# Block 0 of a retention and feed-forward kernel: constants on another queue, rounding units and weight additions in other places, two tiles centred on VectorE

## The chip, the core and the metric

The kernel runs on one core of one Trainium2 chip. A core has TensorE (PE, matmuls, with a sequencer row PEld for weight loads), VectorE (DVE), ScalarE (ACT), GpSimd (POOL) and SyncE (SP), each with its own in-order instruction stream, and 16 DMA engines that serve queues written by SP and ACT. The metric is the device time of one launch in microseconds: the median of several runs. Lower is better.

## The reference

The input is x, 4 sequences of 1024 tokens with 512 features, so 4096 tokens, all float32. Two sandwiched sublayers follow, each wrapped in layer norms without gain:

```python
x = x + LN(attn(LN(x)))
x = x + LN(ffn(LN(x)))

# attn: 16 heads of 32, lam per head
q, v, g = x @ Wq.T, x @ Wv.T, silu(x @ Wg.T)
ret[t]  = lam * ret[t-1] + v[t]              # a scan along the sequence
out     = (LN(q * ret) * gamma + beta) * g
return out @ Wo.T

# ffn: 512 -> 1536 -> 512, weights rounded to float8_e4m3
h = silu((x @ f8(gate_w)) * gate_scale) * ((x @ f8(up_w)) * up_scale)
return (h @ f8(down_w)) * down_scale
```

## The kernel before, in words

**Blocks.** The 4096 tokens are worked through in eight blocks of 512 (t = 0 to 7), each of four tiles of 128 tokens (s = 0 to 3). `Retention` is the attention part of a block, `Ffn` its feed-forward part. The feed-forward loop runs 12 steps (i = 0 to 11) per block: `gate(i)` and `up(i)` are eight matmuls each (`pfg`, `pfu`), `fuse` and `rest` split the product into two parts, `down` adds it into four sums (`pd`). Woven into the steps of block t is the attention part of block t+1 (`b` in the code) and the input of block t+2 (`n`). Every instruction is written in a fixed order per engine and kept in it: the helper `InOrder` records all of them, so the profile gives one line, L74, to all; they are told apart by the names of tiles.

**The first 90 us** are block 0's attention part (`a`), which has no feed-forward work to hide behind. SP and ACT load x in halves, ACT then loads beta and the other constants (`load_const`), SP loads Wv, Wq (`load_square`), four pieces of feed-forward weights, Wg, block 1's x and Wo. On ACT the activation table is loaded behind these issues, and `keep_x` copies the transposed tiles `ptx` to `xnT`, from which the v products (`pv`) start. A DMA takes one of eight semaphores in turn and waits for the DMA eight before it.

**Rounding.** The feed-forward weights are rounded to float8 on the chip, in 18 pieces, from the start until step 7 of block 0. For each piece VectorE takes the exponent bits (`unit`, 128x1024), ScalarE turns them into a rounding constant with two activations (`units()`, a pair), and VectorE adds and subtracts it (`finish`). `rounds(n)` takes n of these VectorE steps; `now=False` leaves the pair of activations to the next call of `units()`. A pair that stands early in ScalarE's order waits for its unit and holds up what is behind it; one that stands late holds up the addition.

**Block 1's statistics.** In step 3 of block 0, `halves()` splits the sum over features (ScalarE the upper half, VectorE the rest), `mean()` multiplies it by ones (`mu`), `center_y()` subtracts and squares, POOL adds the squares (`sqsum`). In step 4 `halves()` and `var()` do the same for the variance (`var`), ScalarE takes the root (`rstd`, with a table load before it), and VectorE the reciprocal. `g_of(c)` is a gate product `pg` with silu.

**x1.** For each tile s, in steps 7 to 11: `o(s)` is the output product (`po`); `o_moments` takes mean and variance (VectorE) and the root (POOL); `x1_of` centres and scales `po` into `x1n`, POOL adds x, SP stores the sum (`kept`); `x1_moments` and `x1n_of` norm it again. Centring goes through `self.center`: `shift_scale` is three ScalarE instructions, `center_scale` is one VectorE instruction. Tiles 0 to 2 of block 1 are then transposed by VectorE blockwise (`xs`), stored by SP in four parts (`mxs`) and fetched back (`x1n<-mxs`); tile 3 is transposed by TensorE (`pt`). `upper_of` (ScalarE) and `rest_of` (VectorE) split the transposed tile into the two parts of `x1nT` that the next block's `pfg` and `pfu` read.

**Weight sums.** From block 2 on, the products with Wv, Wq, Wg go by seven half-size products instead of eight, which need sums of quarters of the weights. `weight_sums(k)` makes them in place with four VectorE additions, `keep_sums(k)` stores the four results to DRAM with four DMAs (`dsum_v`, `dsum_q`, `dsum_g`). Before, this goes in steps 8, 9, 10 for v, q, g: additions ahead of the step's `gate`, stores at its end. When the weights are stored, their places are taken by other tiles: `w_ring` (four slots, filled by `fetch_weights`) lies where `wv_sb` was, `t_sums` (POOL's sums of inputs) where `wq_sb` was, `mids` (intermediate results) where `wg_sb` was. The first product of block 2 is made in step 11 (`product`), the second and third at its end; the first one's result is copied by ScalarE into `mids`, and the third adds into the same bank of results.

The orders that matter for the change, from the end of step 11 in ScalarE's stream: the upper part of tile 2, the cast of `fuse_11`, the copy to `mids`, the upper part of tile 3.

Of the kernel before, what the change touches and what calls it, by code (L numbers as in the profile page):

```python
# [15 lines left out]
ALU = mybir.AluOpType  # L16

P = 128
# [5 lines left out]
def retention_ffn_sandwich(  # L24
# [20 lines left out]
    NT, D = x.shape  # L45
    I = gate_w.shape[1]
    NC = D // P
    NI = I // P
    TB = 512
    NS = TB // P  # L50
# [15 lines left out]
    class InOrder:  # L66


        def __init__(self, engine):
            self.engine = engine  # L70
# [5 lines left out]
    pe, dve, act, pool, sp = (  # L76
        InOrder(e) for e in (nc.tensor, nc.vector, nc.scalar, nc.gpsimd, nc.sync)
    )


    def load_x(t, s, queues):
        xt = xpool.tile([P, D], F32, tag="x", name=f"x_{t}_{s}")
        w = D // len(queues)
        for h, queue in enumerate(queues):
            queue.dma_start(xt[:, ts(h, w)], x[ds(t * TB + s * P, P), ts(h, w)])
        return xt

    x_first = [load_x(0, s, [sp, act]) for s in range(NS)]

    def load_const(src, cols, name):  # L90
        t = const.tile([P, cols], F32, tag=name, name=name)
        act.dma_start(t, src)
        return t

    def load_square(src, name):
        w = wpool.tile([P, NC, D], F32, tag=name, name=name)
        v = src.rearrange("(c p) f -> p c f", p=P)
        for h in range(2):
            sp.dma_start(w[:, 2 * h : 2 * h + 2, :], v[:, 2 * h : 2 * h + 2, :])
        return w  # L100

    beta_sb = load_const(beta, NC, "beta_sb")
    wv_sb = load_square(wvT, "wv_sb")
    wq_sb = load_square(wqT, "wq_sb")
    gamma_sb = load_const(gamma, NC, "gamma_sb")
    lnb_sb = load_const(lnb, NC, "lnb_sb")
    gs_sb = load_const(gate_s, NI, "gs_sb")
    us_sb = load_const(up_s, NI, "us_sb")
    ds_sb = load_const(down_s.to_broadcast([P, D]), D, "ds_sb")


    gate_sb = wpool.tile([P, NC, I], F32R, tag="gate_sb", name="gate_sb")
# [102 lines left out]
    def units():  # L215

        while open_units:
            _, c = open_units.pop(0)
            act.activation(c, c, AF.Relu, bias=neg_low)
            act.activation(c, c, AF.Identity, scale=1.5 * 2.0**20, bias=low_unit)  # L220

    def rounds(n, now=True):
        for _ in range(n):
            next(rounding, None)
            if now:
                units()
# [110 lines left out]
    H = TB // 2  # L337
# [4 lines left out]
    squares = {"v": (wvT, wv_sb), "q": (wqT, wq_sb)}  # L342
    operands = {}

    def weight_sums(k):

        src, w = squares[k]
        v = src.rearrange("(c p) f -> p c f", p=P)
        a11, a12, a21, a22 = (w[:, i : i + 2, o : o + H] for o in (0, H) for i in (0, 2))
        operands[k] = {1: v[:, 0:2, 0:H], 2: v[:, 2:4, 0:H], 4: v[:, 2:4, H:D]}  # L350
        dve.tensor_tensor(a22, a21, a22, ALU.add)
        dve.tensor_tensor(a21, a11, a21, ALU.subtract)
        dve.tensor_tensor(a11, a22, a11, ALU.subtract)
        dve.tensor_tensor(a12, a12, a11, ALU.subtract)
        return {5: a22, 7: a21, 6: a11, 3: a12}

    def keep_sums(k, done):
        for j, t in done.items():
            operands[k][j] = dram.tile([P, 2, H], F32, tag=f"sum_{k}{j}", name=f"dsum_{k}{j}", bufs=1)
            sp.dma_start(operands[k][j], t)  # L360

    RING = 4
# [3 lines left out]
    def fetch_weights():  # L366
        n = fetched[0]
        if n < total_products:
            k, j = order[n % len(order)]
            sp.dma_start(w_ring[:, n % RING], operands[k][j])  # L370
            fetched[0] += 1

    class Retention:


        def __init__(self, t, xt=None):
            self.t = t
            self.xt = xt or [load_x(t, s, [sp]) for s in range(NS)]
            self.mv = small.tile([P, NS, 2], F32, tag="mv4", name=f"mv4_{t}", bufs=2)
            self.pv, self.pq, self.pg, self.ret, self.g = {}, {}, {}, {}, {}  # L380
            self.po, self.mvo, self.x1n, self.ptx, self.kept = {}, {}, {}, {}, {}
            self.center = shift_scale if t < 2 else center_scale
            self.fast = t >= FAST
            self.made = 0

# [278 lines left out]

        def x1_of(self, s):
            self.x1n[s] = work.tile([P, D], F32, tag="tok", name=f"x1n_{self.t}_{s}", bufs=4)
            self.center(self.x1n[s], self.po.pop(s), self.mvo[s])
            pool.tensor_tensor(self.xt[s], self.xt[s], self.x1n[s], ALU.add)
            self.kept[s] = dram.tile([P, D], F32, tag="kept", name=f"kept_{self.t}_{s}")
            sp.dma_start(self.kept[s], self.xt[s])  # L670
# [2 lines left out]
            self.mvo[s] = moments(self.xt[s])  # L673

        def x1n_of(self, s):
            self.center(self.x1n[s], self.xt[s], self.mvo.pop(s))

        def new_x1nT(self):

# [162 lines left out]
        load_piece(n)  # L842
    wg_sb = load_square(wgT, "wg_sb")
    squares["g"] = wgT, wg_sb
    a = Retention(0, x_first)
    a.new_xnT()
    warm(14)
# [113 lines left out]
    a.rest_of(1)  # L961
    b.y_of(0)
    a.rest_of(2)
    rounds(3, now=False)
    a.turn_x1n(3)
    a.upper_of(3)
    b.q(2, "pd0", early)
    units()
    a.rest_of(3)
    b.y_of(1)  # L970


# [3 lines left out]
    for t in range(NB):  # L976
        f, n = Ffn(a), None
        fast = b is not None and b.fast
        for i in range(NI):
# [28 lines left out]
                n.shift()  # L1008
            if b and not fast and i == 5:
                b.z(0)  # L1010
            if b and i >= 8:
                b.x1_moments(i - 8)
            if t == 0 and 8 <= i < 11:
                done = weight_sums("vqg"[i - 8])
            f.gate(i)
            if t == 0 and i in (5, 6):
                n.norm_x(2 * i - 10, True)
# [19 lines left out]
            if b and not fast and i == 3:  # L1037
                b.halves()
                units()
                rounds(3, now=False)  # L1040
                b.g_of(0)
                b.mean()
                b.center_y()
                n.stats(3)
                n.rstd()
                n.shift()
            if b and not fast and i == 4:
                b.halves()
                rounds(3, now=False)
                b.g_of(1)  # L1050
                b.var()
            if b and not fast and i == 5:
# [78 lines left out]
                n.fetch_x()  # L1131
            if b and n and i == 11:
                b.rest_of(3)
            if t == 0 and 8 <= i < 11:
                keep_sums("vqg"[i - 8], done)

            if i == f.lag:
                f.sums()
# [25 lines left out]
                n.stats(1)  # L1164
            if t == 0 and i == 9:
                w_ring = wpool.tile([P, RING, 2, H], F32, tag="wv_sb", name="w_ring")
                for _ in range(RING):
                    fetch_weights()
            if t == 0 and i == 10:
                t_sums = wpool.tile([P, 4, 2, H], F32, tag="wq_sb", name="t_sums")  # L1170
# [76 lines left out]
```

## Time and profile before

| what | value |
|---|---|
| median of 6 runs | 985.28 us (984.5 to 987.72) |
| the profiled execution, its own time | 985.25 us |
| its span (first to last instruction) | 983.4 us |
| TensorE busy | 98% |
| VectorE, ScalarE, POOL busy | 68%, 38%, 27% |
| TensorE busy, 0 to 25 us | 23.28 of 25 |
| VectorE busy, 25 to 75 us | 47.36 of 50 |
| DMA moved | 110.07 MB, 112 GB/s |
| granted TensorE clock, mean | 0.995 |

The profile is one execution. A line of the timeline reads: start in us, duration in us, engine, operation, output and input tiles, shape, count, and in brackets the idle time of the engine before it and what ended it. An SPq line is a DMA issue: its duration is that of the issue, not of the transfer. A line of waits reads: who waited, for whom, total us, times, longest. TensorE's work is counted in pairs of records for float32 matmuls, and ends of matmuls are modelled.

### The profile page before, as it was taken

To read this page: it belongs to the slowest core of one execution; us is meant where nothing else is said; L and a number is where in the kernel's file an instruction comes from. 1 tells how busy PE (TensorE), PEld (TensorE's weight loads), DVE (VectorE), ACT (ScalarE), POOL (GpSimd) and SP (SyncE) were. 2 spreads that over 40 slices of the span, in tenths; PEclk is the share of its full clock that TensorE was granted. 3 is DMA by queue.
4 is the path that set the end of the run, shared out by engine and by line. 5 is a ranking of instruction groups with operands and counts; after the bars stand their busy time and mean duration, and the time that the engine had idled before them with its cause. 6 is when DMAs were issued, how large, how long until landed. Compare 5 with 4: busy or idle time off the path is not lost.

```text
span 983.4 us, 11259 instructions
## 1 busy us (share of the span) xinstructions
PE 964.8 (98%) x3950; PEld 735.6 (75%) x3950; DVE 664.5 (68%) x1019; ACT 369.7 (38%) x556; POOL 265.2 (27%) x346
## 2 busy tenths in 40 slices
PE   9999999999999999999999999999999999999996
PEld 7455766678776888678876788768887788867885
DVE  5996979655666667665686666766667765656535
ACT  3556565466645125221432215321152211522323
POOL 1405121412324033240513305133142312322020
PEclk9999999999999999999999999999999999999998
DMA  9312323752416426263232623245241542213021
GB/s 305 112 65 72 121 65 93 212 177 75 150 53 153 128 81 229 78 142 123 86 129 91 177 76 117 87 132 151 82 150 59 134 139 79 72 43 107 1 86 43
DMA packets 90936, 110.07 MB, mean 112 GB/s; under 512 B 8064, under 2 KB 55424, under 8 KB 90880
## 3 DMA queue, kind: packets, MB, share of 16 engines
q1 hardware_dynamic: 89296, 108.43, 36.2%
q10 hardware_dynamic: 1584, 0.94, 0.3%
q8 instruction: 31, 0.51, 0.2%
q14 instruction: 25, 0.20, 0.1%
HBM read 76.56 MB, written 32.77 MB: 111 GB/s over the span
## 4 chain that ended last, share of the span: by engine, by line
PE 82%; DVE 8%; ACT 4%; POOL 2%; DMA 2%; issue 1%; SPq 1%; ACTq 0%; DVEq 0%; POOLq 0%
PE pfu L74 15%; PE pfg L74 15%; PE pd L74 15%; PE pv L74 10%; PE pq L74 9%; PE pg L74 9%; PE po L74 8%; DVE scr L74 1%; DVE st L74 1%; POOL x L74 1%; POOL mv L74 1%; ACT x1n L74 1%; DVE gate L74 1%; DMA xnT<-mx 1%; DVE xs L74 1%
## 5 line engine op out<-in xcount | busy, mean ns | idle before, releaser
L74 PE MATMUL pfu<-x1nT,up_sb 128*128 128x512 f32 x768 | 212.5, 419 | 0.0
L74 PE MATMUL pfg<-x1nT,gate_sb 128*128 128x512 f32 x768 | 195.2, 396 | 0.4 <-DVE x1nT L74 0.4
L74 PE MATMUL pd<-down_sb,fuse 128*128 128x512 f32 x720 | 186.9, 401 | 0.0
L74 PEld LDWEIGHTS pfu<-x1nT,up_sb 128*128 128x128 f32 x768 | 145.2, 189 | 42.5 <-issue 12.9
L74 PEld LDWEIGHTS pfg<-x1nT,gate_sb 128*128 128x128 f32 x768 | 144.2, 188 | 30.4 <-DVE x1nT L74 0.8
L74 PEld LDWEIGHTS pd<-down_sb,fuse 128*128 128x128 f32 x720 | 135.3, 189 | 27.6
L74 ACT CAST fuse<-gate 128x512 fp32r<-128x512 f32 x90 | 55.7, 619 | 235.0 <-DVE gate L74 235.0
L74 ACT ACTIVATE gate<-pfg,gs_sb 128x512 f32<-128x512 f32 x96 | 65.7, 684 | 195.0 <-PE pfg L74 194.9
L74 DVE SCALAR_TENSOR_TENSOR gate<-pfu,us_sb,gate 128x512 f32<-128x512 f32 x96 | 71.8, 748 | 73.7 <-PE pfu L74 71.2
L74 PE MATMUL po<-wo_sb,y 128*128 128x512 f32 x256 | 114.5, 592 | 0.0
L74 POOL TENSOR_SCALAR mv<-mv 128x1 f32<-128x1 f32 (+1 forms) x82 | 19.4, 237 | 300.6 <-DVE mv L74 299.6
L74 PEld LDWEIGHTS po<-wo_sb,y 128*128 128x128 f32 x256 | 48.2, 189 | 50.3 <-issue 46.6
L74 DVE TENSOR_TENSOR fuse<-gate,fuse 128x512 fp32r<-128x512 f32 x90 | 75.2, 835 | 12.4 <-ACT fuse L74 12.4
L74 POOL TENSOR_TENSOR ysum<-y 128x256 f32<-128x256 f32 (+1 forms) x14 | 14.0, 998 | 190.0 <-DVE y L74 190.0
L74 POOL TENSOR_TENSOR x<-x,x1n 128x512 f32<-128x512 f32 x32 | 46.8, 1461 | 45.7 <-DVE x1n L74 36.8
L74 DVE BATCH_NORM_STATS2 st<-x 128x6 f32<-128x512 f32 x64 | 43.6, 682 | 14.0 <-POOL x L74 11.2
L74 POOL TENSOR_TENSOR mv<-mv,nhalf 128x1 f32<-128x1 f32 (+1 forms) x75 | 46.1, 615 | 6.2
L74 PE MATMUL pg<-t_sums,w_ring 128*128 128x256 f32 x192 | 45.7, 381 | 0.6 <-ACT mids L74 0.6
L74 PE MATMUL pv<-t_sums,w_ring 128*128 128x256 f32 x192 | 45.3, 379 | 0.0
L74 PE MATMUL pq<-t_sums,w_ring 128*128 128x256 f32 x192 | 45.3, 379 | 0.0
L74 PEld LDWEIGHTS pg<-t_sums,w_ring 128*128 128x128 f32 x192 | 35.9, 189 | 7.4 <-ACT mids L74 2.2
L74 PEld LDWEIGHTS pv<-t_sums,w_ring 128*128 128x128 f32 x192 | 36.3, 189 | 5.7
(150 smaller groups left out, 1336.9 us busy)
## 6 DMA issues: line engine op xcount, KB each, us to landing
kept<-x SPq DMA_DIRECT2D x32, 256.0 KB, 2.1
x<-kept SPq DMA_DIRECT2D x32, 256.0 KB, 3.9
x<-in_x SPq DMA_DIRECT2D x28, 256.0 KB, 4.3
out<-d SPq DMA_DIRECT2D x27, 256.0 KB, 2.1
xnT<-mx SPq DMA_DIRECT2D x24, 256.0 KB, 4.7
w_ring<-dsum_v SPq DMA_DIRECT2D x24, 256.0 KB, 2.6
w_ring<-dsum_q SPq DMA_DIRECT2D x24, 256.0 KB, 2.6
w_ring<-dsum_g SPq DMA_DIRECT2D x24, 256.0 KB, 2.6
```

The source lines that it names most:

```text
L74: return lambda *args, **kwargs: tc.keep_in_program_order(op(*args, **kwargs))
```

## The change

Four things are moved, all in block 0's time; the number of matmuls and of additions is the same.

1. The loads of gamma, the norm's beta, the two scales and the down scale (`gamma_sb`, `lnb_sb`, `gs_sb`, `us_sb`, `ds_sb`) go from ACT's queue, where they stood before ACT's first work, to SP's queue, behind Wg and before block 1's x. The retention's beta stays on ACT.
2. Of the three rounding steps before the transpose of tile 3 of block 0, the last (a subtraction) goes behind `a.rest_of(3)`. In steps 3 and 4 of block 0 one more `units()` stands behind `rounds(3)`: the pair of the unit just taken is written before `g_of(0)`, mean and centring in step 3, and before `g_of(1)` and `var` in step 4, where it stood behind them.
3. The 12 additions for weight sums are drawn from one generator: 4 in step 8, 6 in step 9, 2 in step 10, there before `x1_moments(2)`. The g sums are stored at once in step 10 and no longer at its end, so the four DMAs stand before the stores of tile 2's blocks on SP. The ring's first four loads are issued two in step 9 and two in step 10.
4. In block 1, tiles 2 and 3 are centred by `center_scale` on VectorE, both in `x1_of` and in `x1n_of`; tiles 0 and 1 stay on ScalarE.

```diff
-    def load_const(src, cols, name):
+    def load_const(src, cols, name, queue=None):
         t = const.tile([P, cols], F32, tag=name, name=name)
-        act.dma_start(t, src)
+        (queue or sp).dma_start(t, src)
         return t
...
-    beta_sb = load_const(beta, NC, "beta_sb")
+    beta_sb = load_const(beta, NC, "beta_sb", act)
     wv_sb = load_square(wvT, "wv_sb")
     wq_sb = load_square(wqT, "wq_sb")
-    gamma_sb = load_const(gamma, NC, "gamma_sb")
-    lnb_sb = load_const(lnb, NC, "lnb_sb")
-    gs_sb = load_const(gate_s, NI, "gs_sb")
-    us_sb = load_const(up_s, NI, "us_sb")
-    ds_sb = load_const(down_s.to_broadcast([P, D]), D, "ds_sb")
...
-    def weight_sums(k):
-        src, w = squares[k]
...
-        dve.tensor_tensor(a22, a21, a22, ALU.add)
-        dve.tensor_tensor(a21, a11, a21, ALU.subtract)
-        dve.tensor_tensor(a11, a22, a11, ALU.subtract)
-        dve.tensor_tensor(a12, a12, a11, ALU.subtract)
-        return {5: a22, 7: a21, 6: a11, 3: a12}
+    def weight_sums():
+        for k, (src, w) in squares.items():
...
+            made[k] = {5: a22, 7: a21, 6: a11, 3: a12}
+            dve.tensor_tensor(a22, a21, a22, ALU.add)
+            yield
+            dve.tensor_tensor(a21, a11, a21, ALU.subtract)
+            yield
+            dve.tensor_tensor(a11, a22, a11, ALU.subtract)
+            yield
+            dve.tensor_tensor(a12, a12, a11, ALU.subtract)
+            yield
+
+    made = {}
+    adding = weight_sums()
...
-            self.center = shift_scale if t < 2 else center_scale
+            self.center = [shift_scale if t < 1 or t < 2 and s < 2 else center_scale for s in range(NS)]
...
     wg_sb = load_square(wgT, "wg_sb")
     squares["g"] = wgT, wg_sb
+    gamma_sb = load_const(gamma, NC, "gamma_sb")
+    lnb_sb = load_const(lnb, NC, "lnb_sb")
+    gs_sb = load_const(gate_s, NI, "gs_sb")
+    us_sb = load_const(up_s, NI, "us_sb")
+    ds_sb = load_const(down_s.to_broadcast([P, D]), D, "ds_sb")
...
-    rounds(3, now=False)
+    rounds(2, now=False)
     a.turn_x1n(3)
     a.upper_of(3)
     b.q(2, "pd0", early)
     units()
     a.rest_of(3)
+    rounds(1, now=False)
     b.y_of(1)
...
+            if t == 0 and i == 10:
+                for _ in range(2):
+                    next(adding)
+                keep_sums("g")
             if b and i >= 8:
                 b.x1_moments(i - 8)
-            if t == 0 and 8 <= i < 11:
-                done = weight_sums("vqg"[i - 8])
+            if t == 0 and i in (8, 9):
+                for _ in range(4 if i == 8 else 6):
+                    next(adding)
             f.gate(i)
...
             if b and not fast and i == 3:
                 b.halves()
                 units()
                 rounds(3, now=False)
+                units()
                 b.g_of(0)
...
             if b and not fast and i == 4:
                 b.halves()
                 rounds(3, now=False)
+                units()
                 b.g_of(1)
                 b.var()
...
-            if t == 0 and 8 <= i < 11:
-                keep_sums("vqg"[i - 8], done)
+            if t == 0 and i in (8, 9):
+                keep_sums("vq"[i - 8])
...
             if t == 0 and i == 9:
                 w_ring = wpool.tile([P, RING, 2, H], F32, tag="wv_sb", name="w_ring")
-                for _ in range(RING):
+            if t == 0 and i in (9, 10):
+                for _ in range(RING // 2):
                     fetch_weights()
```

More of the change, by code (lines that the diff above doesn't have):

```diff
@@ L343, in retention_ffn_sandwich, with keep_sums @@
     operands = {}
-    def weight_sums(k):
-        src, w = squares[k]
-        v = src.rearrange("(c p) f -> p c f", p=P)
-        a11, a12, a21, a22 = (w[:, i : i + 2, o : o + H] for o in (0, H) for i in (0, 2))
-        operands[k] = {1: v[:, 0:2, 0:H], 2: v[:, 2:4, 0:H], 4: v[:, 2:4, H:D]}
-        dve.tensor_tensor(a22, a21, a22, ALU.add)
-        dve.tensor_tensor(a21, a11, a21, ALU.subtract)
-        dve.tensor_tensor(a11, a22, a11, ALU.subtract)
-        dve.tensor_tensor(a12, a12, a11, ALU.subtract)
-        return {5: a22, 7: a21, 6: a11, 3: a12}
-    def keep_sums(k, done):
-        for j, t in done.items():
+    def weight_sums():
+        for k, (src, w) in squares.items():
+            v = src.rearrange("(c p) f -> p c f", p=P)
+            a11, a12, a21, a22 = (w[:, i : i + 2, o : o + H] for o in (0, H) for i in (0, 2))
+            operands[k] = {1: v[:, 0:2, 0:H], 2: v[:, 2:4, 0:H], 4: v[:, 2:4, H:D]}
+            made[k] = {5: a22, 7: a21, 6: a11, 3: a12}
[9 more added lines that the diff above has]
+    adding = weight_sums()
+    def keep_sums(k):
+        for j, t in made[k].items():
             operands[k][j] = dram.tile([P, 2, H], F32, tag=f"sum_{k}{j}", name=f"dsum_{k}{j}", bufs=1)
@@ L666, in x1_of @@
             self.x1n[s] = work.tile([P, D], F32, tag="tok", name=f"x1n_{self.t}_{s}", bufs=4)
-            self.center(self.x1n[s], self.po.pop(s), self.mvo[s])
+            self.center[s](self.x1n[s], self.po.pop(s), self.mvo[s])
             pool.tensor_tensor(self.xt[s], self.xt[s], self.x1n[s], ALU.add)
@@ L675, in x1n_of @@
         def x1n_of(self, s):
-            self.center(self.x1n[s], self.xt[s], self.mvo.pop(s))
+            self.center[s](self.x1n[s], self.xt[s], self.mvo.pop(s))
         def new_x1nT(self):
```

## The prediction

> **What bounds the kernel now.** I read the page first, then the list of what TensorE waited for, then all engines in order of time from 120 to 205 us, then the same places of a later block, which already runs part of what the change does.
>
> From the page, the busy times:
>
> ```profile
> PE 964.8 (98%) x3950; PEld 735.6 (75%) x3950; DVE 664.5 (68%) x1019; ACT 369.7 (38%) x556; POOL 265.2 (27%) x346
> ```
>
> TensorE is the bound nearly everywhere. An edit in block 0 can only win idle time of TensorE there; the work behind it moves as one. TensorE's waits from 0 to 205 us (total, times, longest):
>
> ```profile
> PE pt L74 <- ACT x1n L74: 2.4, 2, 2.1
> PE pv L74 <- ACT xnT L74: 1.8, 2, 1.2
> PE var L74 <- ACT half L74: 1.4, 1, 1.4
> PE pv L74 <- ACT mids L74: 1.1, 1, 1.1
> ...
> PE pfg L74 <- DVE x1nT L74: 0.4, 1, 0.4
> PE var L74 <- DVE half L74: 0.2, 1, 0.2
> ```
>
> That is some 7 us, of which the change touches 5.8 (0.68, 0.37, 1.60, 2.08, 1.09). The places in order of time, from the timelines of TensorE, ScalarE, SyncE and TensorE again (start, duration, work, idle before and its releaser):
>
> ```profile
> 9.39 1.99 PE L74 MATMUL pv<-xnT,wv_sb 128*128 128x256 f32 x8 [0.68 <-ACT xnT L74]
> ...
> 95.63 1.88 PE L74 MATMUL pfg<-x1nT,gate_sb 128*128 128x512 f32 x7 [0.37 <-DVE x1nT L74]
> ...
> 129.88 0.50 PE L74 MATMUL var<-half,mean_r 128*128 128x512 f32 x1 [1.38 <-ACT half L74]
> ...
> 134.91 3.34 DVE L74 RECIPROCAL rstd<-rstd 128x512 f32<-128x512 f32 x1
> ...
> 190.72 1.91 SPq L74 DMA_DIRECT2D mxs<-xs  x4
> 195.05 0.34 SPq L74 DMA_DIRECT2D x1n<-mxs  x1
> ...
> 195.91 3.05 SPq L74 DMA_DIRECT2D dsum_g<-wg_sb  x4
> ...
> 197.13 0.66 PE L74 MATMUL pt<-ident,x1n 128*128 128x128 f32 x4 [2.08 <-ACT x1n L74]
> ...
> 201.84 0.58 ACT L74 COPY mids<-pv 128x512 f32<-128x512 f32 x1 [2.87 <-DMA w_ring<-in_wvT]
> ```
>
> Between 90 and 165 us VectorE is nearly full (9.83 of 10 us in 150 to 160), so a gain of TensorE there lives on only if VectorE's chain comes earlier too. The last line names a load, but `mids` lies where `wg_sb` was: the copy waits for the four stores of the g sums to land (last issue about 197.9, 3.6 us to landing). After 202.5 us TensorE's small waits (0.64 at 253, 0.28 at 315) follow from its own results, so what is won or lost by 202.5 us is won or lost for the whole.
>
> **The change, part by part.** Times are those of the profiled execution: span 983.4, own time 985.25, 0.03 under the median 985.28, so differences carry over as they are.
>
> *Constants' loads.* Five issues leave ScalarE's queue, where they run from 4.51 to 6.85 and hold up the table load (6.88, 1.28 us) and with it the first two copies (1.05 us from 8.29). Now the table load follows beta at about 4.2, the second copy starts at the end of its transpose (7.66+0.60=8.26) and takes 0.53, and `pv` starts at 8.85 for 9.39: 0.54 us won. On SP the five (0.33 to 0.44 each, 2.0 in sum) stand ahead of block 1's x, first read at 37.1 and loaded by then with 10 us to spare (issued by 18.6, at most 9.6 to landing); the constants are read from 58 us on. SP also loses a wait of 2.8 us for beta, which held Wq back to 8.27. TensorE has no gap from there to 50, so the 0.54 stays.
>
> *`rest_of(3)` before the last subtraction.* It now starts when its upper half is copied (93.93) instead of 94.89. The eight `pfg` matmuls take 94.87 to 97.51, 2.64 us, against 1.81 undisturbed: 0.85 won. Behind it `y_of(1)` ends 0.26 later (96.35), which nobody awaits: `gate_0` waited 0.31 for TensorE. TensorE is then 1.39 early, and VectorE, which waited 0.99 and 0.31 for it, follows by 107 us.
>
> *Rounding pairs in block 1's steps 3 and 4.* A pair is 1.13+1.15 us on ScalarE. In step 3 it fills a hole (ScalarE idle 3.23 before the squares): the unit is out at 118.25, the pair ends at 120.55, silu at 121.1, the first square starts at 121.29 as y allows. The cast that waited behind the old pair goes ahead, the upper half of the sum is made at 126.65, bound by POOL's three additions (128.04 less 1.39), and `var` starts at 127.3 for 129.88: TensorE is 2.6 early. It also ran at half clock just behind that gap (0.50 in 132 to 134), some 1.3 us. [...] In step 4 the new pair stands *ahead* of silu, table load and root: unit 128.55, pair to 130.9, silu 131.4, table 132.7, root 133.4. The reciprocal, which nothing else would hold after `gate_4` (131.6), starts at 133.4 for 134.91. VectorE's chain keeps only 1.5, and the half clock falls inside what VectorE makes TensorE wait anyway: `gate_5`'s silu (142.35 for 143.85) releases `pfg_6`.
>
> *Additions 4, 6, 2 for 4, 4, 4.* Four take 2.84, so 0.71 each. With 1.5 won the moments of x1 tile 1 end at 174.8, six additions at 179.05, and the transpose of tile 1 goes at 179.05 for 179.29: 1.25 of the 1.5 is spent.
>
> *Centring tiles 2 and 3 on VectorE.* ScalarE's three steps (0.20+0.29+0.78) and its waits go; VectorE gets two of 0.80 and two of 0.55, counting from a later block:
>
> ```profile
> 428.52 0.80 DVE L74 TENSOR_SCALAR x1n<-po,mv 128x512 f32<-128x512 f32 x1
> ...
> 429.84 1.78 DVE L74 TENSOR_TENSOR fuse<-gate,fuse 128x512 fp32r<-128x512 f32 x1
> ...
> 433.39 1.47 DVE L74 TENSOR_SCALAR x1n<-x,mv 128x512 f32<-128x512 f32 x1 [0.95 <-POOL mv L74]
> ```
>
> The second and third show the price: beside POOL's x addition (429.40 to 431.07) a 0.69 us operation takes 1.78, and beside POOL's `t_sums` the 0.55 centring takes 1.47. Working on: po_2's moments 179.7, gate 181.2, cast 181.9, `rest_9` 182.5, centring 183.3, POOL's x 185.0; the two g additions are caught behind it, to 186.3 (uncaught 185.2). Then moments of tile 2 at 186.3 (were 184.77), centring to 188.7, transpose, po_3 at 189.4, `rest_10` 191.65, centring 193.0, POOL to 194.7, moments, centring 196.55 to 198.0 beside `t_sums`. So `pt` goes at 198.05, not 197.13, and the second product behind it, 4.1 us of TensorE later, at 202.1. [...]
>
> *The g sums' stores ahead of tile 2's blocks.* The wait of 1.09 us goes: the stores are issued by 192.9 and land by 196.5. But SP is a queue: stored x1 of tile 2 (185.0), four q stores (2.90), two ring loads (1.49), four g stores (3.05), so tile 2's block stores go at 192.9 for 190.72. From there to the fetch took 3.94 and 4.33 in this stage and 6.39 in a later block; at 4.33, the row with the same stores before it, the fetch is issued at 197.2 and lands 2.8 later, 200.0 (was 197.83). On ScalarE the upper half of tile 2 waits for it, and behind that stand `fuse_11` (0.53), the `mids` copy (0.58) and tile 3: 0.6+0.53+0.58 puts `pv` at 201.75 for 202.48. The third and fourth ring loads, issued behind the fetch at 198, land by 201.8 and are just in time.
>
> **Sum.** Two chains meet at 202: `pt` and its followers 202.1, `mids` 201.8. The later sets it: 202.1 less 202.48, -0.4 us, 984.9. [...] Bounds: with the catching at nothing (1.1 at the additions, 0.9 at the last centring) `pt` goes at 196.05, and at 3.94 to the fetch the second chain gives 201.35: -1.1. With 6.39 it is 203.9, +1.4. If the first 0.54 fails because Wv's second half (up to 10.1) holds `pv`, add 0.5.
>
> **The rivals.** *Faster: both chains carry the 1.5 to the end.* It needs the additions and centrings free beside POOL, and SP through early: tile 2's x stored at 183.3, blocks at 191.2, fetch 195.1 landing 197.9, `mids` 199.65, and `pt` at 195.6 with its product at 199.7: -2.8, 982.5. For it: ScalarE's six small steps and their waits on POOL are gone, and in 166.97 to 169.8 the additions ran at 0.71 beside POOL's small operations. Against it: the rows of 1.78 and 1.47. If TensorE kept all it won by 142 us (2.75) and lost both waits (2.08, 1.09) too, 5.9 would be won, 979.4; VectorE's chain forbids that.
>
> *Slower: SP's queue.* Its place is the g stores ahead of tile 2's blocks. At the slowest single issue (1.10, four are 4.4 for 3.05) and 6.39 to the fetch, the second chain comes 3.4 later, at 205.2: +2.7, 988.0. It decides once tile 2 lands after 202.7, 4.9 later than before. For it: these stores and loads put 2.5 MB into the queue within 7.5 us, 333 GB/s, and the transfers there already move some 340. Against: the stores before tile 1's blocks left 3.94.
>
> *No effect:* the edits act, but waits they leave stand in the same place; that is the forecast's neighbourhood.
>
> **How the numbers follow.** 0.2% is 1.97 us, about what a measurement of this kernel tells from no change. Forecast within it 0.44 (983.3 to 987.2; its own range 983.9 to 986.7), faster 0.36, slower 0.20. The faster share is large because each estimate leans on contention rows that need not recur at the same overlap; the slower share is the queue and a half clock (1.3 us) behind TensorE's gap before 202, now some 2 us. Range 981.8 to 987.6: it cuts about 0.1 off each side.
>
> **What would show it.** Right: the table load near 4.2 and `pv` near 8.85; no gap before `pfg` at 95; `var` near 127.3 and the reciprocal near 133.4; transpose of tile 1 near 179; block stores of tile 2 near 193; `mids` waiting behind tile 2's upper half, not behind the g stores; `pv`'s wait gone to that or to `pt`. Wrong: tile 2 landing by 198, or `pt` before 196 (then faster); `mids` after 204 (slower); a TensorE gap after 205 that was not there.

## The result, and the profile after

The changed kernel took 987.63 us (median of 18 runs, 986.47 to 988.92) where the kernel before took 985.21 (36 runs, 984.35 to 987.72): ratio 1.0023, 95% interval 1.0017 to 1.003. It is slower by 2.4 us between the medians. The forecast was 984.9 with a range to 987.6, so the time lies just outside it and on the wrong side. The profiled execution of the changed kernel took 986.88, span 984.9. It is 0.75 under its kernel's median, so its trace shows 1.6 of the 2.4 us.

TensorE's busy time is what it was, as the page's first part says:

```profile
PE 964.5 (98%) x3950; PEld 735.1 (75%) x3950; DVE 668.7 (68%) x1023; ACT 365.0 (37%) x544; POOL 266.7 (27%) x346
```

ScalarE lost 4.7 us of work and VectorE gained 4.2. So the loss is idle time of TensorE, or matmuls at a lower clock. TensorE's waits from 0 to 205 us in the changed kernel (total, times, longest):

```profile
PE pt L74 <- DVE x1n L74: 3.4, 1, 3.4
PE pfu L74 <- DVE gate L74: 1.7, 1, 1.7
PE pfg L74 <- ACT gate L74: 1.4, 1, 1.4
PE pv L74 <- ACT xnT L74: 1.4, 2, 1.2
...
PE var L74 <- ACT half L74: 0.6, 1, 0.6
```

Four of the waits aimed at are shorter or gone (`var` 0.6 for 1.4, `pv` 1.4 for 1.8, `pfg` behind the rest of tile 3, `mids`), and three long ones have come in their place. All three wait for VectorE or ScalarE in the stretch from 142 to 200 us. The last of them, in the timeline of TensorE:

```profile
192.11 2.12 PE L74 MATMUL pfu<-x1nT,up_sb 128*128 128x512 f32 x8 [1.73 <-DVE gate L74]
...
199.38 1.09 PE L74 MATMUL pt<-ident,x1n 128*128 128x128 f32 x4 [3.43 <-DVE x1n L74]
200.12 3.05 PE L74 MATMUL pd<-down_sb,fuse 128*128 128x512 f32 x8
203.01 1.89 PE L74 MATMUL pv<-t_sums,w_ring 128*128 128x256 f32 x8
204.74 1.89 PE L74 MATMUL pv<-xnT,w_ring 128*128 128x256 f32 x8
```

`pt` starts 2.25 us later than before, and the four transposes take 1.09 for 0.66, the eight `pd` 3.05 for some 2.1. The windows say why (columns: window, length, TensorE busy, granted clock, DMA share, GB/s):

```profile
196.00:198.00 2.00, 0.00 (x0) 1.00 0.31 81
198.00:200.00 2.00, 0.61 (x3) 0.69 0.82 262
200.00:202.00 2.00, 2.00 (x8) 0.50 0.73 212
202.00:204.00 2.00, 2.00 (x10) 0.95 0.52 186
```

The clock was halved behind the gap. Before, all four windows stand at 1.00. So the last product of block 0 (the third, `pv` from `xnT`, which waited for `mids` before) starts at 204.74 for 202.48, 2.26 later. A wait of 0.28 at 315 us is gone afterwards, which leaves 1.85, and 1.5 in the span.

**Where the early gains went.** TensorE is 0.85 early at `pfu_1`, the up product of step 1 (104.89 for 105.74), and 1.14 early from 154 to 188. Up to 0.44 of either is no gain of the change: x landed that much earlier in this execution (VectorE's first work on it starts at 3.37 for 3.81). VectorE is not early. Its reciprocal:

```profile
132.25 0.75 DVE L74 SCALAR_TENSOR_TENSOR gate<-pfu,us_sb,gate 128x512 f32<-128x512 f32 x1
134.83 3.35 DVE L74 RECIPROCAL rstd<-rstd 128x512 f32<-128x512 f32 x1 [1.83 <-ACT rstd L74]
```

It starts 0.08 earlier than before, although the product in front of it is 2.0 earlier: it now waits 1.83 for the root. ScalarE's stream at that place shows what the root stands behind:

```profile
129.97 1.15 ACT L74 ACTIVATE scr<-scr,neg_low 128x1024 f32<-128x1024 f32 x1 [1.36 <-DVE scr L74]
131.16 1.16 ACT L74 ACTIVATE scr<-scr,low_unit 128x1024 f32<-128x1024 f32 x1
132.22 0.58 ACT L74 ACTIVATE g<-pg 128x512 f32<-128x512 f32 x1
132.81 1.28 ACT L74 ACT_TABLE_LOAD   x1
134.11 0.69 ACT L74 ACTIVATE rstd<-var,eps_sb 128x512 f32<-128x512 f32 x1
```

The first two lines are the pair that step 4 now writes ahead. From there VectorE is where it was before (147.92 for 147.99 at the next addition), with two more additions to make ahead of tile 1's transpose and four more centrings ahead of `pt`.

The theory to be tested (A in the expectations) had three parts: the pair of step 4 spends what was won early; additions and centring then push `pt` back on VectorE; and TensorE, which had stayed early, makes a gap of it that lowers its clock. The main rival was the one of the forecast, SP's queue.

### The profile page after: what moved, and what is told of

It reads as the page before. It is cut to its first block, busy times and chain, and to the rows that moved or that the text cites. A ratio compares the mean times of both kernels' runs of the same rounds, so it can differ in the third digit from the quotient of the medians.

```text
span 984.9 us, 11255 instructions
## 1 busy us (share of the span) xinstructions
PE 964.5 (98%) x3950; PEld 735.1 (75%) x3950; DVE 668.7 (68%) x1023; ACT 365.0 (37%) x544; POOL 266.7 (27%) x346
## 4 chain that ended last, share of the span: by engine, by line
PE 87%; DVE 7%; ACT 2%; POOL 1%; DMA 1%; issue 1%; SPq 0%; ACTq 0%; DVEq 0%; POOLq 0%
PE pfu L74 16%; PE pfg L74 16%; PE pd L74 16%; PE pq L74 10%; PE pv L74 10%; PE po L74 10%; PE pg L74 9%; DVE scr L74 1%; DVE st L74 1%; PE pt L74 1%; DVE fuse L74 1%; DMA wv_sb<-in_wvT 1%; POOL sqsum L74 1%; DVE y L74 1%; DVE d L74 1%
```

## The experiments

All times are medians beside runs of the kernel before on the same chip (985.4 to 985.7 in the three sets); the ratios are to those, with 95% intervals. The start of the kernel shifts by up to a microsecond between profiled executions: x lands at 3.37 to 3.81, and the wait for Wv differs. So the reciprocal of the changed kernel's own stream lies between 134.83 and 135.80 in the variants that leave the first 150 us alone. Places are therefore compared by the distance between two instructions of one execution.

**Undoing the centring.**

```diff
-self.center = [shift_scale if t < 1 or t < 2 and s < 2 else center_scale for s in range(NS)]
+self.center = [shift_scale if t < 2 else center_scale] * NS
```

> The changed kernel with tiles 2 and 3 centred on ScalarE again; the rest of the change stays. Theory A (the loss is made by VectorE's chain in steps 9 to 11, half of it by the centring, and is doubled by a half clock behind a TensorE gap of 3.43 us): the transpose pt goes at 198.4 for 199.38, so 986.6 if the half clock stays (0.50 behind the gap) and 985.2 if the shorter gap (2.4 us) leaves the clock full. Theory B (SP's queue, with the g stores ahead of tile 2's blocks, holds the end): the third product does not move, 987.6.

Measured: 986.15, ratio 1.0004 (0.9996 to 1.0013). `pt` at 198.34 behind a gap of 2.32, clock 1.00 there, so most of the loss is gone. But the third product came at 203.55, behind a new wait of 0.97. The fetch of tile 2 was issued only at 198.32 (197.26 in the changed kernel) and landed by 201.4. The profile puts the wait down to ScalarE's upper part of tile 3, done at 203.51, right behind the `mids` copy (203.02); the ring load issued behind the fetch landed at 203.41. All three stand behind that fetch, so SP's queue does then become the bound, one step after VectorE's.

**Undoing the moved additions and stores.**

```diff
-            if t == 0 and i == 10:
-                for _ in range(2):
-                    next(adding)
-                keep_sums("g")
...
-            if t == 0 and i in (8, 9):
-                for _ in range(4 if i == 8 else 6):
+            if t == 0 and 8 <= i < 11:
+                for _ in range(4):
```

(The stores go back to the ends of the steps, the four ring loads to step 9.)

> The changed kernel with additions, g stores and ring loads where they stood before (four additions in each of steps 8, 9, 10, stores at the steps' ends); centring of tiles 2 and 3 stays on VectorE. Theory A (centring on VectorE beside POOL costs most): x1 moments of tile 2 go at 185.2, pt at 199.0, the wait for mids comes back behind it, 987.0. Theory B (the two extra additions and SP's queue are the loss): 985.3, pt at 198 or before.

Measured: 988.17, ratio 1.0018 (1.001 to 1.0027): nothing is won. `pt` stands 64.05 behind the reciprocal, 0.50 less than in the changed kernel, but behind a gap of the same length (3.42), and the half clock lasted 6.8 us in this profile. The wait for `mids` that theory A expected did not come.

**Leaving out the pair of step 4.**

```diff
                 b.halves()
                 rounds(3, now=False)
-                units()
                 b.g_of(1)
                 b.var()
```

> The changed kernel without the extra pair of step 4, so root and table load no longer stand behind it on ScalarE. Theory A (the early gains of 1.1 us are lost at the reciprocal, which starts at 134.83 for 134.91 since the root waits for that pair): the reciprocal goes at 132.9, gate_5's silu 1.9 earlier, TensorE's wait of 1.40 before pfg_6 goes, VectorE's chain and pt come 1.9 earlier, 985.7. Theory B (VectorE is full from 150 to 170 or waits for POOL and DMA there, so nothing early arrives): pt stays at 199.4, 987.6.

Measured: 985.16, ratio 0.9995 (0.9986 to 1.0004), 2.5 us under the changed kernel. The reciprocal starts at once behind its product, and the wait of 1.4 for `gate_5` is gone. By its start (133.86) it is 0.97 earlier, which looks like half of what I expected, but this execution was 0.95 later already at `pfu_1` and at `var` (129.61 for 128.66), ahead of the edit. From `var` to the reciprocal it takes 4.25 where the changed kernel takes 6.17: the pair costs 1.92, as expected, and `pt` keeps it (92.61 behind `pfu_1` for 94.49). That is most of the 2.5 between the medians. `pt` waited 3.42 in this profile too, but the clock behind it was 1.00.

**Filling the gap.** Small matmuls of constants, into the bank that `pt` overwrites; the first variant did it in six blocks, the second in block 0 only:

```diff
                 n.product()
-                b.turn_x1n(3, "pf")
+                if t == 0:
+                    pt = ps_tile("pt1_fill", "pf")
+                    for _ in range(14):
+                        pe.matmul(pt[:, :P], mean_w, mean_w, start=True, stop=True)
...
```

> The changed kernel with 14 small matmuls of constants (128x128) in TensorE's gap before pt, written to the bank that pt then overwrites; they do not touch any result. Theory A (the clock falls to 0.50 at 198.6 because of the gap and stretches the transposes, pd and pv): pt stays at 199.4, the clock behind it is 1.00, pd takes 2.1 for 3.05, 986.3. Theory B (pd is stretched by something else, such as late weights): the clock and pd stay as they are, 987.6 or more.

Measured: 1000.63, ratio 1.015 (1.0135 to 1.0165). The edit was wrong: 14 matmuls take 3.29 us, and five later blocks have no gap to put them in. In block 0 itself the run did what theory A said (third product at 203.76, clock 1.00).

> The changed kernel with the 14 small matmuls of constants before pt in block 0's step 11 only (the run with them in six blocks paid some 3.3 us for each of the later five). Theory A (behind the gap of 3.43 us the clock falls to 0.50 in most executions, and costs 1.0): third product at 203.8 for 204.74, 986.6, clock 0.998, and executions that lie closer together. Theory B (the clock is an accident of one execution): 987.5, spread as it was (986.5 to 988.9).

Measured: 986.29, ratio 1.0007 (0.9999 to 1.0016), 11 runs from 986.04 to 987.43, mean clock 0.997 or 0.998 in each. TensorE in this run:

```profile
196.41 3.29 PE L74 MATMUL pt_fill<-mean_r 128*128 128x128 f32 x28
199.91 0.66 PE L74 MATMUL pt_fill<-ident,x1n 128*128 128x128 f32 x4 [0.21 <-DVE x1n L74]
...
203.95 1.89 PE L74 MATMUL pv<-xnT,w_ring 128*128 128x256 f32 x8
```

`pt` waits for the same VectorE work, but from `pt` to the third product it takes 4.04 us (199.91 to 203.95) for 5.36 in the changed kernel. The half clock costs 1.32 in a profile that has it, and 0.16% in the ratios (1.0023 to 1.0007; the intervals just do not touch).

**The early part alone**, without the pair of step 4 and with additions, stores and centring as before:

> Constants, rest_of(3) and the pair of step 3 as in the changed kernel; the pair of step 4, the additions and the centring as in the kernel before. Theory A (without the pair of step 4 VectorE is 1.05 early at 147 and keeps it to the end, with no new work in steps 9 to 11): third product at 201.4 for 202.48, 984.3 where before has 985.4. Theory B (what is won early is lost at the last wait, since mids waits for stores on SP's queue): third product at 202.4, as before.

Measured: 984.04, ratio 0.9987 (0.9978 to 0.9996): faster than before. The reciprocal at 133.21, `pt` at 195.43. The third product did not follow:

```profile
195.43 0.66 PE L74 MATMUL pt<-ident,x1n 128*128 128x128 f32 x4 [1.92 <-ACT x1n L74]
...
202.13 3.60 PE L74 MATMUL pv<-xnT,w_ring 128*128 128x256 f32 x8 [2.48 <-ACT mids L74]
```

So the trace has theory B's wait (202.13 for 202.4), while the median is what theory A gave (984.04 for 984.3). The profiled execution is the slowest of the 11 (986.03), and the half clock behind this gap, with 3.60 for the eight matmuls of the third product (1.99 before), is most of what it lies above the median. SP issued tile 2's fetch at 194.72, only 0.33 earlier than in the kernel before, though the blocks were stored 1.42 earlier; the g sums' stores stand behind it.

**Centring alone**, on the kernel before:

> The kernel before with tiles 2 and 3 centred on VectorE, and nothing else of the change. Theory A (centring costs by itself: in one queue with the weight additions and beside POOL's additions): pt at 198.9 for 197.13, a TensorE gap of about 3 us, 986.4 with a full clock behind it and 987.6 with a half one. Theory B (centring is harmless, the loss needs the six additions and the moved stores): pt at 197.1, 985.4.

Measured: 987.32, ratio 1.0018 (1.0009 to 1.0027). This one edit makes nearly the whole loss, with the same signs: `pt` at 199.13 behind 3.39 of idle time, then half clock for 6.8 us (`pd` 3.76; the profile is that of the slowest of 11 executions, 988.57):

```profile
199.13 1.09 PE L74 MATMUL pt<-ident,x1n 128*128 128x128 f32 x4 [3.39 <-DVE x1n L74]
199.87 3.76 PE L74 MATMUL pd<-down_sb,fuse 128*128 128x512 f32 x8
```

**The eight `pd` ahead of `pt`** in block 0, in the changed kernel: the gap filled with work that is due anyway.

```diff
                 n.product()
-                b.turn_x1n(3, "pf")
-                b.upper_of(3)
+                if t:
+                    b.turn_x1n(3, "pf")
+                    b.upper_of(3)
...
+            if b and n and i == 11 and t == 0:
+                b.turn_x1n(3, "pf")
+                b.upper_of(3)
+                b.rest_of(3)
             if n and i == 11:
                 n.products(2)
```

> The changed kernel with one order turned, in block 0's step 11 only: the eight pd matmuls, which are ready, stand before the transpose of tile 3 instead of behind it (and so the upper part and the rest of tile 3 behind them). Theory A (TensorE idles 3.43 us for pt and then runs at half clock): pd fills 2.1 us of the gap, the clock stays full, pt at 199.4, third product at 202.2, pfg of block 1 at 204.5 for 206.28, bound by the rest of tile 3 on VectorE, 985.8. Theory B (other waits at 202 to 206 hold the same end): 987.5.

Measured: 986.08, ratio 1.0007 (0.9998 to 1.0016). The wait for `pt` is 1.60, the clock 1.00 throughout, and the third product stands 67.46 behind the reciprocal (69.91 in the changed kernel, 67.57 before).

**All early edits, with the pair of step 4**, without the rest:

> All the early edits, the pair of step 4 included; additions, stores and centring as in the kernel before. Beside the run without that pair (984.04) this prices the pair of step 4 alone. Theory A (it holds the root, and so the reciprocal, back by all that was won): reciprocal 2.0 to 2.3 us after the gate product of step 4, VectorE at 148 as in the kernel before, pt at 197, behind a TensorE gap that is now 1.1 longer (3.1 us), so 985.2 with a full clock and 986.3 with a half one. Theory B (the pair costs nothing where no centring and no six additions follow): 984.0.

Measured: 985.83, ratio 0.9999 (0.9991 to 1.0008), for 0.9987 without the pair (intervals overlap a little). From `var` to the reciprocal it takes 6.17 with the pair and 4.25 without it, the same 1.92 as above. With the pair:

```profile
128.21 0.50 PE L74 MATMUL var<-half,mean_r 128*128 128x512 f32 x1 [0.58 <-ACT half L74]
...
131.80 0.75 DVE L74 SCALAR_TENSOR_TENSOR gate<-pfu,us_sb,gate 128x512 f32<-128x512 f32 x1
134.38 3.35 DVE L74 RECIPROCAL rstd<-rstd 128x512 f32<-128x512 f32 x1 [1.83 <-ACT rstd L74]
```

Without it:

```profile
128.96 0.50 PE L74 MATMUL var<-half,mean_r 128*128 128x512 f32 x1 [0.60 <-ACT half L74]
...
132.55 0.74 DVE L74 SCALAR_TENSOR_TENSOR gate<-pfu,us_sb,gate 128x512 f32<-128x512 f32 x1
133.21 3.34 DVE L74 RECIPROCAL rstd<-rstd 128x512 f32<-128x512 f32 x1
```

`pt` follows: it stands 92.20 behind `pfu_1` with the pair, 90.29 without it. (By their starts the two are 1.17 apart, since the first execution was 0.75 ahead at `var`.) That one pair undoes the early part. The gap was 2.29, not 3.1: TensorE was itself held 0.33 and 1.4 on the way.

**Additions and stores alone**, on the kernel before:

> The kernel before with the additions in 4, 6, 2, the g stores at once in step 10 and the ring's loads in two halves, and nothing else. Theory A (two more additions of 0.7 delay tile 1's and po_2's work by 1.3, and the g stores delay tile 2's blocks on SP): pt at 198.3 for 197.13, tile 2 landing 3 us later than before, third product at 203.4 for 202.48, 986.3. Theory B (the moved stores pay, since mids no longer waits for them): third product at 201.7, 984.6.

Measured: 986.52, ratio 1.0009 (1.0 to 1.0018). In its stream six additions stand in a row, and the tile's transpose behind them no longer waits for the centring:

```profile
175.50 2.83 DVE L74 TENSOR_TENSOR wq_sb<-wq_sb 128x512 f32<-128x512 f32 x4
178.25 1.41 DVE L74 TENSOR_TENSOR wg_sb<-wg_sb 128x512 f32<-128x512 f32 x2
179.58 0.71 DVE L74 STREAM_TRANSPOSE xs<-x1n 128x512 f32<-128x512 f32 x1
```

`mids` no longer waits for the stores; theory B's part is true, but `pt` is 1.15 later after the reciprocal, and its gap of 2.50 brought a half clock here. The two additions that step 10 no longer has gave nothing back (17.91 from tile 1's transpose to `pt`, 17.84 before).

**A version that beats both.** The early part without the pair of step 4, four additions in each step and centring on ScalarE; of the late edits only the g stores at once behind their additions, with the ring's loads split:

```diff
             if t == 0 and 8 <= i < 11:
                 for _ in range(4):
                     next(adding)
+                if i == 10:
+                    keep_sums("g")
...
-                for _ in range(RING):
+            if t == 0 and i in (9, 10):
+                for _ in range(RING // 2):
                     fetch_weights()
```

> The early edits without the pair of step 4, four additions in each step, ScalarE centring, and in step 10 the g stores at once behind their additions, ahead of tile 2's blocks on SP, with the ring's loads in two halves. Theory A (SP is a queue, so what the stores win tile 2's blocks lose, and mids stands behind tile 2's upper half on ScalarE): tile 2 lands at 199.3, mids copied at 201.0 for 201.5, 983.6. Theory B (only the stores' landing held mids): third product at 200 for 202.1, 982.3.

Measured: 982.92, ratio 0.9971 (0.9959 to 0.9982), 982.50 to 983.39 in 6 runs: 2.5 us under before, and by the two ratios 0.52% under the changed kernel. The copy to `mids` starts at 199.40 and TensorE goes on at 200.85:

```profile
195.75 0.66 PE L74 MATMUL pt<-ident,x1n 128*128 128x128 f32 x4 [2.50 <-ACT x1n L74]
...
200.85 1.96 PE L74 MATMUL pv<-xnT,w_ring 128*128 128x256 f32 x8 [0.87 <-DMA w_ring<-in_wvT]
```

So SP's queue, the mechanism of my slower rival, cost little here: the fetch stands 61.93 behind the reciprocal for 61.51 without the moved stores, and the copy to `mids` 65.89 for 68.28. Now a ring load ends the wait.

**The same stores from ScalarE's queue:**

```diff
             f.gate(i)
+            if t == 0 and i == 11:
+                keep_sums("g", act)
```

> The early edits without the pair of step 4, four additions in each step, ScalarE centring, and the four g stores issued by ScalarE in step 11 behind gate_11 instead of by SP. Theory A (the stores then stand behind nothing, 191.5 to 194, and land by 197; tile 2's fetch on SP stays): mids copied at 199.3, third product at 199.7 for 202.1, pfg of block 1 at 201.5 for 204, 982; ScalarE's centring of tile 3 is held back by at most 1 us. Theory B (the transfers themselves are the bound, not the queue that issues them): mids at 201, 984.0.

Measured: 984.63, ratio 0.9989 (0.998 to 0.9997); the copy to `mids` starts at 201.01. SP in this run:

```profile
191.50 3.97 SPq L74 DMA_DIRECT2D mxs<-xs  x4
```

Tile 2's four block stores are held to 191.50, though their transpose was done at 188.0, and take 3.97 from the first to the last (1.91 before), so the fetch, at 197.19, stands 1.62 further behind the reciprocal than from one queue. Theory B was nearer. The four issues themselves take 0.32 to 0.47 each. SP waited 2.2 for a ring load to land ahead of the first, and 2.3 for one of the g stores ahead of the second: it was held by earlier DMAs still in flight.

## Why the prediction was wrong, by its steps

Five distances carry it (us, each within one execution; the third product is block 0's last):

| kernel | `pfu_1` to `var` | `var` to reciprocal | reciprocal to transpose of tile 1 | that transpose to `pt` | `pt` to third product |
|---|---|---|---|---|---|
| before | 24.14 | 5.03 | 44.38 | 17.84 | 5.35 |
| forecast | 22.95 | 6.10 | 45.65 | 19.00 | 4.1 |
| changed | 23.77 | 6.17 | 45.46 | 19.09 | 5.36 |
| additions and stores alone | 24.13 | 4.25 | 45.46 | 17.91 | 5.57 |
| centring alone | 24.13 | 4.24 | 44.38 | 19.66 | 6.83 |
| centring undone | 23.82 | 6.18 | 45.47 | 17.90 | 5.21 |
| pair of step 4 left out | 23.77 | 4.25 | 45.47 | 19.12 | 4.02 |
| early part alone | 23.82 | 4.25 | 44.37 | 17.85 | 6.70 |
| all early edits | 23.81 | 6.17 | 44.38 | 17.84 | 5.85 |

**The step that failed: "TensorE is then 1.39 early, and VectorE, which waited 0.99 and 0.31 for it, follows by 107 us."** TensorE was 0.85 early there. `rest_of(3)` gave 0.59 of its 0.85 (10.47 from the first `pfg` to `pfu_1` for 11.06). The constants gave nothing that the traces show: `pfg` was 0.26 early in an execution whose x landed 0.44 early; it stands 90.5 to 91.8 behind x in the runs with the loads moved, and 90.9 to 92.2 in the three without. Here the second half of `pv` waited 0.27 for Wv and started at 10.00, the bound I had named. VectorE took up less still, since it was busy with work of its own. One exponent step took 1.40 for 1.02 and another 1.10 for 0.68, both beside POOL's additions to `ysum`, and the sum's rest (`half`) was 0.44 early at 117.95, no more. POOL's three additions, which I had ending at 126.65, ended at 127.96, and `var` came at 128.66, not 127.3. That is 1.36 late, 0.54 of it by `pfu_1`.

**The pair of step 4 was priced right, and the miss went on through it: "The reciprocal ... starts at 133.4."** From `var` to the reciprocal I had 6.10, and it took 6.17; the runs with and without the pair price it at 1.92 in both cases. So the reciprocal started at 134.83, 1.43 late, almost all of it from `var`. Of the 1.5 that the sum carried to the end, 0.08 was there.

**What the steps after the reciprocal cost was right.** Two more additions ahead of tile 1's transpose cost 1.08, whatever else is there. Centring costs 1.82 alone and 1.18 with the additions; together they push `pt` 2.33 back, 0.64 less than their sum. The rows beside POOL came as counted: the two g additions took 2.51 for 1.4, the last centring 1.47 for 0.55. Why VectorE takes longer there no run shows; the sum rests on the times alone. With the late reciprocal these distances put `pt` at 199.38 where I had 198.05: 1.33 later.

**The step left out of the sum: the clock.** I wrote that the following product comes 4.1 us of TensorE behind `pt`, and put "a half clock (1.3 us) behind TensorE's gap" into the slower share alone. I also took the gap to be about 2 us; it was 3.43, since `pt` was late while TensorE was early. The stretch took 5.36, 1.3 more. The two errors are the whole miss at the third product: -0.38 forecast, +1.33 and +1.3, and 2.26 was measured.

Against the kernel before, this half clock is less a new loss than one in another place. The mean granted clock of the changed kernel's 18 executions is 0.9957, that of the kernel before in the three sets 0.9958 to 0.9961, where one half clock of 3.41 us is 0.0017. In the profile of the kernel before it falls at 131 to 135 us.

**SP's queue went as the sum had it, and the slower rival did not occur.** Block stores at 193.35 (forecast 192.9), fetch at 197.26 (197.2), upper half of tile 2 at 200.17 (200.0), `mids` copied by 201.79 (201.75), and TensorE's wait for `mids` gone. My slower case gave 988.0, near the measured time, but by luck: its condition, tile 2 landing after 202.7, did not occur.

**The half clock at 132 us** is gone, as forecast, with the shorter wait before `var`. I held it to lie inside other waits. In the kernel before it delays the up product of step 4 and so the reciprocal: the run with additions and stores alone happened to have full clock there, and its reciprocal started at 134.12 for 134.91, from the same first product (`pv` at 9.38 and 9.39).

What stays open: the constants and `rest_of(3)` were tried only together with the pair of step 3, so their single shares are read from the trace alone, and so is the reason why VectorE did not follow TensorE.

## What to carry to other kernels

A gain on the engine that is the bound is kept only if the engine it next waits for is early too; otherwise it turns into a longer gap at the next meeting point, and a longer gap can cost clock on top (here 1.32 us behind one of 3.43). Here VectorE, nearly full, took up 0.44 of TensorE's 0.85. When an instruction is written ahead of others in an in-order stream, look first at the work it holds up: here 2.3 us of rounding, for an addition that could wait, stood ahead of a root that could not, at a price of 1.92 (1.8 by the forecast's own numbers, 133.4 for 131.6). Parts of one change deserve single runs: here one late edit of several was worth keeping, and dropping the others and the pair of step 4 turned 0.23% slower into 0.29% faster.

## What the runs showed of the hardware

Where the half clock appeared it lasted 3.41 us (198.78 to 202.19 in the changed kernel; the same in the kernel before and in the runs with the early part and with the additions alone) or twice that, 6.83, in the two runs with four additions in step 10 and centring on VectorE. It began 2.1 to 2.9 us after TensorE fell idle, so that it may meet work that has started again (in the kernel before it came at 131.38, 1.50 after `var`).

The length of the gap does not decide it alone. Gaps of 3.43, 3.42 and 3.39 were followed by it, another of 3.42 was not; of three gaps of 2.48 to 2.50 two were and one was not; one of 1.38 was, and another of 1.38 at the same place was not (the run with additions and stores alone); those of 1.92, 2.08, 2.29, 2.32 and 2.40 (the last in the run with ScalarE's stores) were not. What else decides it the runs do not show. For a forecast it means that a gap such as these before dense work (the half clock followed six of the 14 named) should be priced at the chance of a half clock (1.32 us here, when it falls), in the sum and not only in the range.
